# Context values of four heads in one run of products, tokens on partitions

## The chip, the cores and the metric

The kernel runs on one core of one Trainium2 chip. The metric is the device time of one execution in microseconds (us). The kernel before took 2483.2 us, the median of 3 runs (2482.09 to 2486.21).

## What is computed

One post-norm decoder layer in float32 over x of 8 batches x 100 tokens x 1024 features: a retention block, a cross attention over the layer's own tokens and a context of 722 tokens a batch, and a gated feed-forward block, each followed by a residual sum and a layer norm. The change lies in the cross attention, of which this is the core:

```python
q = (x @ wq).reshape(B, L, 16, 128)
k = (x @ wk).reshape(B, L, 4, 128)
v = (x @ wv).reshape(B, L, 4, 128)
k_ctx = (h_ctx_kv @ wk_ctx).reshape(B, 722, 4, 128)
v_ctx = (h_ctx_kv @ wv_ctx).reshape(B, 722, 4, 128)
...
k_full = jnp.concatenate([k_ctx, k], axis=1)
v_full = jnp.concatenate([v_ctx, v], axis=1)
scores = jnp.einsum('blhd,bmhd->bhlm', q, k_full) * scale + mask
probs = jax.nn.softmax(scores, axis=-1)
out = jnp.einsum('bhlm,bmhd->blhd', probs, v_full)
```

Four query heads share one of the four key/value heads, so keys and values are repeated four times ahead of the scores. Keys and queries are also RMS-normalised, and own queries and keys rotated.

## The kernel before

Activations lie with features on the 128 partitions and tokens along the row. Every float32 operand of a product is kept as a high part and a low part in the type fp32r, and `mm3` (L89) makes a product of three matmuls: high x high (L90), high x low (L93) and low x high (L94). `split2` (L67) makes the two parts: ScalarE (ACT) copies into fp32r and VectorE (DVE) subtracts, both on L68. `proj` (L113) multiplies a 128-column block of weights by all 8 blocks of features: 24 matmuls into one bank of PSUM. Banks come by tag: three of `a`, four of `s`, one of `v` (L51).

The program is written as a sequence; a scheduler then sets the order of instructions on each engine, from a timeline of its own, with the buffers of the pools as limits. A tile with `bufs=1` can be written again only when all its readers are done. On each engine the order is then fixed.

Stage one is the retention block. At its side `core` (L538) prepares the weights of the context for all later batches: `wc` holds, by turns, the key and value weights of the four heads; each is split into high and low part and kept in DRAM as `wcd` (1 MB each, L565 by SP's queue; L566 adds on POOL's queue, to complete the low part).

A stage of queries, own keys and own values follows, and at its side the context of batch 0 is loaded and the context keys of heads 0 and 1 of batch 0 are made (`early`, L723 to L759). The queries are kept in `qd`, the own keys in `kd`, the own values in `vd`.

Then comes the loop that the change is in, over 8 batches `b` and 4 key/value heads `kv` (L773 to L870). For one batch:

- `load_context` (L689) loads the context in 8 pieces (`cs`, 3 buffers) and splits them into four tiles `cz`, in two halves of 362 and 360 tokens (`SH`, L21). The four tiles hold the context of one batch; the next batch's come in when the last product has read them.
- `context_keys` (L693): one head's weights by `load_ws` (L82, tag `w`, four buffers of 1 MB), a product for each half, ACT's square (L705), POOL's sum over partitions (L706, 2.4 us), and the split into `kall`, which has two buffers. The sums go to DRAM as a row (L710) and come back as a column (L800); L802 to L809 make from it a scale `rk` for each context token.
- `context_values` (L713): one head's weights, a product for each half with features on partitions, copied out of PSUM (L719, once by ACT and once by DVE), turned by TensorE in six transposes (L794), and split into `vall` (L796), two tiles that heads use by turns. Own values come in behind the context's (L785, L786).
- The scores (L821) for 822 keys in seven chunks c of 128 keys with 4 x 100 queries along the row, in the order 6, 5, 0, 1, 2, 3, 4; chunk 5 is the context's last 82 keys and the first own ones, chunk 6 the own rest. ACT (L828) or DVE (L824) scale them into `s`; DVE takes the maximum over chunks (L829, L832) and POOL over partitions (`all_red`, L833).
- The softmax: DVE subtracts the maximum (L839, L843), ACT takes the exponential (L845), `split2` makes `ph` and `pl`, DVE sums over chunks (L848, L851), and POOL over partitions (L852). `s`, `ph` and `pl` have one buffer each.
- The context product (L858): 21 matmuls into bank `v` with `vall` as weights; then the division by the sum (L862 to L867), a split and a store to `o2d` (L870).

After the loop `out_proj` (L238) multiplies by the output weights, in two halves of the batches, adds the residual and normalises. Its first half (batches 0 to 3) can begin before the loop's end. Its tile `y` and its residual tiles `rs` are in pool `y2`, which opens before the loop (L764).

Of the kernel before, what the change touches and what calls it, by code (L numbers as in the profile page):

```python
# [8 lines left out]
F32 = mybir.dt.float32  # L9
FR = mybir.dt.float32r  # L10
AF = mybir.ActivationFunctionType
ALU = mybir.AluOpType
# [4 lines left out]
P = 128  # L17
B, T, D = 8, 100, 1024
NB = 4
N = NB * T  # L20
KT = D // P  # L21
QT = KT // 2
SC, SH = 722, 362
SN = [SH, SC - SH]
NC = 7
ORDER = (6, 5, 0, 1, 2, 3, 4)
C5 = SC - 5 * P
R6 = SC + T - 6 * P
# [3 lines left out]
NKV = 4  # L32
# [8 lines left out]
def decoder_layer(ctx, tc, xT, cT, w1, wo1, w2, wo2, wc, w3, wd, gw, qw, kw, trig, dec, mask, out):  # L41
    nc = tc.nc

    def sbuf(name, bufs, side=None):
        return tc.tile_pool(name=name, bufs=bufs, side=side, reuse_waits="tile")
# [8 lines left out]
    def bank(tag):  # L54
        return ps.tile([P, 512], F32, tag=tag, name=tag, bufs=banks[tag])

    def f32(ap):
        return ap.bitcast(F32)

    def bt(ap):  # L60
        return ap.rearrange("p (b t) -> p b t", b=NB)
# [5 lines left out]
    def split2(hi, lo, src):  # L67
        return nc.scalar.copy(hi, src), nc.vector.tensor_tensor(lo, src, f32(hi), ALU.subtract)  # L68
# [10 lines left out]
            split(w, st)  # L79
        return w  # L80

    def load_ws(i):  # L82
        w = wp.tile([P, 2, KT * P], FR, tag="w", name="w", bufs=4)
        nc.sync.dma_start(out=f32(w), in_=f32(wcd[i]))
        return w

    pin = tc.keep_in_program_order
# [1 line left out]
    def mm3(acc, lh, ll, rh, rl, start, stop, chain=False, pinned=False):  # L89
        i = nc.tensor.matmul(acc, lh, rh, start=start, stop=False, skip_group_check=chain)  # L90
        if pinned:
            pin(i)
        nc.tensor.matmul(acc, lh, rl, start=False, stop=False, skip_group_check=chain)  # L93
        nc.tensor.matmul(acc, ll, rh, start=False, stop=stop, skip_group_check=chain)  # L94
# [18 lines left out]
    def proj(w, z, n=N, tag="a", todo=None, pinned=False):  # L113
        acc = bank(tag)[:, :n]
        first = pinned
        for k in range(KT):
            pinned = between(todo, k) or first and k == 0
            t = z[k // QT]
            mmw(acc, w, k, t[:, 0, k % QT, :n], t[:, 1, k % QT, :n], k == 0, k == KT - 1, pinned)
        return acc  # L120
# [53 lines left out]
    o2d = dr.tile([B, P, NKV, 4, 2, T], FR, name="o2d")  # L174
    zd = dr.tile([2, P, KT, N], F32, name="zd")
    zd2 = dr.tile([2, P, KT, N], F32, name="zd2")
    wcd = dr.tile([2 * NKV, P, 2, KT * P], FR, name="wcd")
    hd = dr.tile([QT - 1, 7, P, 2, QT, N], FR, name="hd")
    h3d = dr.tile([4, P, 2, QT, N], FR, name="h3d")

# [296 lines left out]
    with sbuf("l1", 2) as p:  # L477
# [60 lines left out]
        def core(h):  # L538

            for half in range(2):  # L540
                q, k = qk[half, 0], qk[half, 1]
                pf = p.tile([T, NB, T], F32, tag="pf", name="pf")
                s = bt(bank("v")[0:T, :N])
                for b in range(NB):
                    e = slice(b * T, (b + 1) * T)
                    nc.tensor.matmul(s[:, b], k[:, e], q[:, e], start=True, stop=True)
                nc.vector.tensor_tensor(pf, s, dcy[:, h, None, :].to_broadcast([T, NB, T]), ALU.mult)
                ot = p.tile([P, 2, N], F32, tag="ot", name="ot")
                sq = p.tile([P, 2, N], F32, tag="sq", name="sq", bufs=1)
                for blk in range(2):  # L550
                    vv = v[half, blk]
                    o = bank("s")[:, :N]
                    for b in range(NB):
                        nc.tensor.matmul(bt(o)[:, b], vv[:, b * P:(b + 1) * P], pf[:, b], start=True, stop=True)  # L554
                    nc.scalar.activation(ot[:, blk], o, AF.Copy, scale=gws[:, blk:blk + 1])
                    nc.scalar.activation(sq[:, blk], o, AF.Square)
                nc.vector.tensor_tensor(sq[:, 0], sq[:, 0], sq[:, 1], ALU.add)
                oo[half], ss[half] = ot, all_red(p, sq[:, 0], "ss")


            w = wp.tile([P, 2, KT * P], FR, tag="w", name="w", bufs=4)
            st = load_raw(wc[h])
            nc.scalar.copy(w[:, 0], st)
            nc.scalar.activation(w[:, 1], f32(w[:, 0]), AF.Copy, scale=-1.0)
            nc.sync.dma_start(out=f32(wcd[h]), in_=f32(w))  # L565
            nc.gpsimd.dma_start(out=f32(wcd[h])[:, 1], in_=st, accum_op=ALU.add)  # L566

        def gated(h, g):

# [97 lines left out]
    cz = []  # L667
# [21 lines left out]
    def load_context(b):  # L689
        for _ in context_steps(b, wp, 3):  # L690
            pass

    def context_keys(kv):  # L693

        kall = ka.tile([P, 2, SC + T], FR, tag="kall", name="kall")
        wk = load_ws(2 * kv)
        sq = ka.tile([P, SC], F32, tag="ksq", name="ksq", bufs=1)
        ss = ka.tile([P, 6 * P], F32, tag="kss", name="kss", bufs=1)
        row = dr.tile([6, P], F32, tag="row", name="row", bufs=2)
        nc.gpsimd.memset(ss[:, SC:], 1.0)  # L700

        def step(hf):
            n, at = SN[hf], slice(hf * SH, hf * SH + SN[hf])
            acc = proj(wk, cz[hf], n)
            nc.scalar.activation(sq[:, at], acc, AF.Square)  # L705
            nc.gpsimd.partition_all_reduce(ss[:, at], sq[:, at], P, RED.add)  # L706
            nc.scalar.activation(kall[:, 0, at], acc, AF.Copy, scale=kws)
            nc.vector.scalar_tensor_tensor(kall[:, 1, at], acc, kws, f32(kall[:, 0, at]), ALU.mult, ALU.subtract)
            if hf:
                nc.sync.dma_start(out=row.rearrange("c p -> (c p)")[None, :], in_=ss[0:1])  # L710
        return step, (kall, row)

    def context_values(kv):  # L713

        wv = load_ws(2 * kv + 1)
        vt = ka.tile([P, SC], F32, bufs=1, tag="cvt", name="cvt")
        for hf in range(2):
            copy = nc.scalar.copy if hf == 0 else nc.vector.tensor_copy
            copy(vt[:, hf * SH:hf * SH + SN[hf]], proj(wv, cz[hf], SN[hf]))  # L719
        return vt  # L720


    early = []  # L723
    behind = list(behind)
    groups = [[(kv, 5) for kv in range(NKV)]]
    for kv in range(NKV):
        groups += [[(kv, i) for i in range(2)], [(kv, i) for i in range(2, 5)]]
    unit = NKV
    with sbuf("l2", 2) as p:
        ctx0 = context_steps(0, p, 2, behind)  # L730
# [30 lines left out]
    z1pool.__exit__(None, None, None)  # L761


    y2pool = sbuf("y2", 1)  # L764
    y2p = y2pool.__enter__()
    with sbuf("cx", 2) as p, sbuf("c1", 1) as p1:

        ph = p1.tile([P, NC, N], FR, name="ph")
        pl = p1.tile([P, NC, N], FR, name="pl")
        valls = [p1.tile([P, NC, 2, P], FR, name=f"vall{i}") for i in range(2)]  # L770
        for t in [ph[:, 0], pl[:, 0]] + [v[:, 6] for v in valls]:
            nc.gpsimd.memset(f32(t), 0.0)
        for b in range(B):  # L773
            if b > 0:
                load_context(b)
            for kv in range(NKV):
                if early:
                    kall, row = early.pop(0)
                else:
                    step, (kall, row) = context_keys(kv)  # L780
                    step(0)
                    step(1)
                nc.sync.dma_start(out=f32(kall[:, :, SC:]), in_=f32(kd[kv, :, b]))
                vall = valls[kv % 2]
                nc.sync.dma_start(out=f32(vall[C5:P, 5]), in_=f32(vd[kv, 0:P - C5, b]))  # L785
                nc.sync.dma_start(out=f32(vall[0:R6, 6]), in_=f32(vd[kv, P - C5:T, b]))  # L786
                q = p.tile([P, 4, 2, T], FR, tag="q", name="q")
                nc.sync.dma_start(out=f32(q).rearrange("p h l t -> p h (l t)"),
                                  in_=f32(qd[kv, :, :, b]).rearrange("h p l t -> p h (l t)"))
                vt = context_values(kv)  # L790
                for c0, c1, rows in ((0, 3, P), (3, 5, P), (5, 6, C5)):
                    tr = bank("s")
                    for c in range(c0, c1):
                        nc.tensor.transpose(tr[0:rows, (c - c0) * P:(c - c0 + 1) * P], vt[:, c * P:c * P + rows], ident)  # L794
                    src = tr[0:rows, 0:(c1 - c0) * P].rearrange("p (c d) -> p c d", d=P)
                    split2(vall[0:rows, c0:c1, 0], vall[0:rows, c0:c1, 1], src)  # L796

                rr = p.tile([P, 6], F32, tag="rr", name="rr")
                with nc.allow_non_contiguous_dma("a row turned into a column"):
# [8 lines left out]
                nc.vector.scalar_tensor_tensor(rk[:, 0:5], r1[:, 0:5], 3.0, r0[:, 0:5], ALU.subtract, ALU.mult)  # L808
                nc.vector.scalar_tensor_tensor(rk[0:C5, 5:6], r1[0:C5, 5:6], 3.0, r0[0:C5, 5:6], ALU.subtract, ALU.mult)  # L809

                s = p1.tile([P, NC, N], F32, tag="s", name="s")
                mx = p.tile([P, N], F32, tag="mx", name="mx")
                def part(ap, c):
                    ap = bt(ap)
# [39 lines left out]
                for j in (1, 0, 2, 3, 4, 5, 6):  # L854
                    c = ORDER[j]
                    n = N6 if c == 6 else N
                    o = bt(ov)[:, :, T6:] if c == 6 else bt(ov)
                    mm3(o, vall[:, c, 0], vall[:, c, 1], bt(ph[:, j, :n]), bt(pl[:, j, :n]),  # L858
                        j == 1, j == NC - 1)

                r = p.tile([P, N], F32, bufs=1, tag="r0", name="r0")
# [10 lines left out]
    def load_o2(half):  # L872
# [4 lines left out]
                in_=f32(o2d[half * NB:(half + 1) * NB, :, g]).rearrange("b p h l t -> p b (h l t)"))  # L877
        return lambda k: (t[k // 4][:, :, k % 4, 0], t[k // 4][:, :, k % 4, 1])

    kapool.__exit__(None, None, None)  # L880


# [384 lines left out]
```

## Time and profile before

| | before |
|---|---|
| median of 3 runs | 2483.2 us |
| profiled execution | 2485.66 us |
| its span | 2483.9 us |
| TensorE clock granted | 0.997 of full |
| loop over batches and heads, first to last softmax | some 832 to 1604 us of the span |
| VectorE busy over the span | 79% |
| ScalarE busy over the span | 54% |
| GpSimd busy over the span | 19% |

The span is from the first to the last instruction; the rest of the execution's time lies around it. In lines of instructions the name left of the arrow is written and those right of it are read; a number in square brackets is the time that the engine stood idle before the instruction, with what ended it. Matmuls are pipelined: one is shown with 0.33 us though the next starts after half of that, so a price is read from one start to the next. PE is TensorE, SP the queue that issues most DMAs. In a table by windows the columns are the stretch, its length, then busy time and instructions of PE, PE's weight loads, DVE, ACT and POOL, the granted clock, the share of the DMA engines and GB/s.

### The profile page before, as it was taken

What the parts mean: (1) busy time and instruction counts of PE and PEld (TensorE: products, weight loads), DVE (VectorE), ACT (ScalarE), POOL (GpSimd) and SP (SyncE); (2) the same over time, 40 slices, a digit from 0 to 9 for tenths busy, and PEclk for the clock granted to TensorE, in tenths of its full rate; (3) what the DMA queues carried; (4) which work ended last, traced back from release to release, by engine and by line L of the source; (5) the groups of instructions that cost most, each with busy time, mean ns of one, the idle gap of its engine ahead of it and who ended that gap; (6) DMA issues with size and microseconds to landing.
All of it is one profiled execution on the core that took longest, in us unless ns stands there. A gap on an engine that the chain in (4) does not pass through costs nothing.

```text
span 2483.9 us, 37221 instructions
## 1 busy us (share of the span) xinstructions
PE 2459.2 (99%) x14068; PEld 2440.1 (98%) x14068; DVE 1953.3 (79%) x3101; ACT 1340.1 (54%) x2258; POOL 460.2 (19%) x234
## 2 busy tenths in 40 slices
PE   9999999999999999999999999999999999999997
PEld 9999999999999999999999999999999999999997
DVE  7777877566898698998998999748978777666756
ACT  6667676334888465666566656534545445432221
POOL 0111111000565333443443433100000000000000
PEclk9999999999999999999999999999999999999999
DMA  7333445775544555455555454565445444389731
GB/s 244 112 111 129 134 141 185 247 261 181 164 161 157 182 175 168 144 181 159 160 174 159 152 181 168 165 241 178 154 174 194 163 161 161 121 301 324 267 103 54
DMA packets 224451, 433.98 MB, mean 175 GB/s; under 512 B 47338, under 2 KB 168042, under 8 KB 211854
## 3 DMA queue, kind: packets, MB, share of 16 engines
q1 hardware_dynamic: 222542, 426.87, 51.2%
q0 software_dynamic: 1152, 4.19, 1.1%
q8 instruction: 111, 1.82, 0.3%
q14 instruction: 70, 0.57, 0.1%
q10 hardware_dynamic: 576, 0.52, 0.1%
HBM read 322.18 MB, written 109.35 MB: 174 GB/s over the span
## 4 chain that ended last, share of the span: by engine, by line
PE 93%; DVE 3%; DMA 2%; ACT 1%; issue 1%; SPq 0%; DVEq 0%; ACTq 0%
PE a L94 20%; PE a L93 20%; PE a L90 20%; PE s L94 9%; PE s L93 9%; PE s L90 9%; PE v L94 2%; PE v L90 2%; PE v L93 1%; PE s L554 1%; PE s L794 1%; PE s L166 1%; DVE y L331 0%; DMA cs<-in_cT 0%; DMA rs<-zd 0%
## 5 line engine op out<-in xcount | busy, mean ns | idle before, releaser
L90 PE MATMUL a<-big,w 128*128 128x400 f32 (+2 forms) x1808 | 609.8, 338 | 0.9 <-DVE y L424 0.7
L93 PE MATMUL a<-big,w 128*128 128x400 f32 (+2 forms) x1808 | 609.2, 337 | 0.2 <-DVE big L68 0.2
L94 PE MATMUL a<-big,w 128*128 128x400 f32 (+2 forms) x1808 | 608.0, 337 | 0.6 <-DVE w L68 0.6
L68 ACT CAST w<-wst 128x1024 fp32r<-128x1024 f32 (+1 forms) x231 | 239.6, 1039 | 386.2 <-PE s L94 146.0
L68 DVE TENSOR_TENSOR w<-wst,w 128x1024 fp32r<-128x1024 f32 (+1 forms) x231 | 280.6, 1215 | 135.0 <-ACT w L68 133.0
L90 PEld LDWEIGHTS a<-big,w 128*128 128x128 f32 x1808 | 340.0, 188 | 2.4 <-DVE y L424 1.0
L93 PEld LDWEIGHTS a<-big,w 128*128 128x128 f32 x1808 | 340.5, 188 | 1.6 <-DVE big L68 0.4
L94 PEld LDWEIGHTS a<-big,w 128*128 128x128 f32 x1808 | 340.7, 189 | 1.5 <-DVE w L68 0.9
L90 PE MATMUL a<-z,w 128*128 128x400 f32 x680 | 234.7, 345 | 0.4 <-ACT w L68 0.4
L93 PE MATMUL a<-z,w 128*128 128x400 f32 x680 | 234.7, 345 | 0.0
L94 PE MATMUL a<-z,w 128*128 128x400 f32 x680 | 234.5, 345 | 0.0
L90 PE MATMUL s<-big,w 128*128 128x400 f32 x664 | 230.0, 347 | 0.1
L94 PE MATMUL s<-big,w 128*128 128x400 f32 x664 | 228.9, 346 | 0.4 <-DVE w L68 0.4
L93 PE MATMUL s<-big,w 128*128 128x400 f32 x664 | 229.2, 345 | 0.0
L141 POOL PARTITION_ALL_REDUCE ss<-sq x56 | 148.4, 2651 | 325.8 <-DMA vd<-vs 185.6
L706 POOL PARTITION_ALL_REDUCE kss<-ksq x64 | 166.1, 2596 | 125.3 <-ACT ksq L705 124.6
L828 ACT ACTIVATE s<-s,rk 128x400 f32<-128x400 f32 x160 | 88.1, 591 | 101.1 <-DVE sm L848 66.7
L90 PEld LDWEIGHTS a<-z,w 128*128 128x128 f32 x680 | 127.6, 188 | 1.2 <-ACT w L68 0.8
L94 PEld LDWEIGHTS a<-z,w 128*128 128x128 f32 x680 | 128.4, 189 | 0.0
L93 PEld LDWEIGHTS a<-z,w 128*128 128x128 f32 x680 | 127.6, 188 | 0.4
L90 PEld LDWEIGHTS s<-big,w 128*128 128x128 f32 x664 | 124.6, 188 | 1.7 <-ACT w L68 0.4
L94 PEld LDWEIGHTS s<-big,w 128*128 128x128 f32 x664 | 125.1, 188 | 0.7 <-DVE w L68 0.7
(355 smaller groups left out, 5444.4 us busy)
## 6 DMA issues: line engine op xcount, KB each, us to landing
wst<-in_w SPq DMA_DIRECT2D x135, 512.0 KB
w<-wcd SPq DMA_DIRECT2D x64, 1024.0 KB
wst<-in_wo SPq DMA_DIRECT2D x64, 512.0 KB
hd<-h SPq DMA_DIRECT2D x12, 1400.0 KB
wst<-in_wd SPq DMA_DIRECT2D x64, 256.0 KB
big<-o1d SPq DMA_DIRECT2D x16, 800.0 KB
qd<-d SPq DMA_DIRECT2D x32, 400.0 KB
q<-qd SPq DMA_DIRECT2D x32, 400.0 KB
```

The source lines that it names most:

```text
L68: return nc.scalar.copy(hi, src), nc.vector.tensor_tensor(lo, src, f32(hi), ALU.subtract)
L90: i = nc.tensor.matmul(acc, lh, rh, start=start, stop=False, skip_group_check=chain)
L93: nc.tensor.matmul(acc, lh, rl, start=False, stop=False, skip_group_check=chain)
L94: nc.tensor.matmul(acc, ll, rh, start=False, stop=stop, skip_group_check=chain)
L141: nc.gpsimd.partition_all_reduce(y, x, P, op)
L166: nc.tensor.transpose(tr[0:T, b * P:(b + 1) * P], vt[:, b * T:(b + 1) * T], ident)
L554: nc.tensor.matmul(bt(o)[:, b], vv[:, b * P:(b + 1) * P], pf[:, b], start=True, stop=True)
L706: nc.gpsimd.partition_all_reduce(ss[:, at], sq[:, at], P, RED.add)
L794: nc.tensor.transpose(tr[0:rows, (c - c0) * P:(c - c0 + 1) * P], vt[:, c * P:c * P + rows], ident)
L828: nc.scalar.activation(sc, sp, AF.Copy, scale=rk[:, c:c + 1])
```

## The change

The values of the context are made for all four heads of a batch at once, before the first head. For each chunk of 128 context tokens the context is the stationary operand and the value weights of the four heads, side by side, are the moving one: 8 blocks of features x 3 matmuls with 512 columns fill one bank with tokens on partitions and four heads x 128 features along the row. The split goes from there into `vall`; there is no copy and no transpose. For this

- the two halves of the context become 384 and 338 tokens, so that a half holds three whole chunks;
- stage one writes the value weights of a head into `wvd`, with the four heads of a feature block next to each other, in runs of 128 values; the key weights stay in `wcd`, four of them;
- a batch loads its value weights as four tiles, each with two feature blocks of all four heads, in the four buffers of tag `w`; the key weights of head 0 come into a buffer of their own, `wk`;
- `vall` is one tile for the four heads of a batch, 28672 bytes a partition, where there were two with 7168 each;
- pool `y2` opens after the loop, not before it;
- the last pair of groups of the stage before runs in the opposite order, and `s` is taken once before the loop.

```diff
-SC, SH = 722, 362
+SC, SH = 722, 384
...
-    def load_ws(i):
-        w = wp.tile([P, 2, KT * P], FR, tag="w", name="w", bufs=4)
-        nc.sync.dma_start(out=f32(w), in_=f32(wcd[i]))
+    def load_ws(src, w=None):
+        if w is None:
+            w = wp.tile([P, 2, KT * P], FR, tag="w", name="w", bufs=4)
+        nc.sync.dma_start(out=f32(w), in_=f32(src))
         return w
...
-    wcd = dr.tile([2 * NKV, P, 2, KT * P], FR, name="wcd")
+    wcd = dr.tile([NKV, P, 2, KT * P], FR, name="wcd")
+    wvd = dr.tile([P, 2, KT, NKV, P], FR, name="wvd")
...
-            nc.sync.dma_start(out=f32(wcd[h]), in_=f32(w))
-            nc.gpsimd.dma_start(out=f32(wcd[h])[:, 1], in_=st, accum_op=ALU.add)
+            if h % 2 == 0:
+                to, wf, low = f32(wcd[h // 2]), f32(w), st
+            else:
+
+                to, wf = f32(wvd)[:, :, :, h // 2], f32(w).rearrange("p l (k n) -> p l k n", n=P)
+                low = st.rearrange("p (k n) -> p k n", n=P)
+            nc.sync.dma_start(out=to, in_=wf)
+            nc.gpsimd.dma_start(out=to[:, 1], in_=low, accum_op=ALU.add)
...
-    def context_values(kv):
-
-        wv = load_ws(2 * kv + 1)
-        vt = ka.tile([P, SC], F32, bufs=1, tag="cvt", name="cvt")
-        for hf in range(2):
-            copy = nc.scalar.copy if hf == 0 else nc.vector.tensor_copy
-            copy(vt[:, hf * SH:hf * SH + SN[hf]], proj(wv, cz[hf], SN[hf]))
-        return vt
+    def context_values(vall):
+
+        wv = [load_ws(wvd[:, :, 2 * j:2 * j + 2].rearrange("p l k v n -> p l (k v n)")) for j in range(QT)]
+        for c in range(NC - 1):
+            rows, hf, at = C5 if c == 5 else P, c // 3, c % 3 * P
+            acc = bank("a")[0:rows, :NKV * P]
+            for k in range(KT):
+                zh, zl = (cz[hf][k // QT][:, l, k % QT, at:at + rows] for l in range(2))
+                wh, wl = (wv[k // 2][:, l, k % 2 * NKV * P:(k % 2 + 1) * NKV * P] for l in range(2))
+                mm3(acc, zh, zl, wh, wl, k == 0, k == KT - 1)
+            split2(vall[0:rows, c, :, 0], vall[0:rows, c, :, 1], acc.rearrange("p (v d) -> p v d", d=P))
...
-        groups += [[(kv, i) for i in range(2)], [(kv, i) for i in range(2, 5)]]
+        pair = [[(kv, i) for i in range(2)], [(kv, i) for i in range(2, 5)]]
+        groups += pair[::-1] if kv == NKV - 1 else pair
...
-        valls = [p1.tile([P, NC, 2, P], FR, name=f"vall{i}") for i in range(2)]
+        vall = p1.tile([P, NC, NKV, 2, P], FR, name="vall")
...
             if b > 0:
                 load_context(b)
+            context_values(vall)
             for kv in range(NKV):
                 if early:
                     kall, row = early.pop(0)
                 else:
-                    step, (kall, row) = context_keys(kv)
+                    w = p1.tile([P, 2, KT * P], FR, tag="wk", name="wk") if kv == 0 else None
+                    step, (kall, row) = context_keys(kv, w)
...
-                vall = valls[kv % 2]
-                nc.sync.dma_start(out=f32(vall[C5:P, 5]), in_=f32(vd[kv, 0:P - C5, b]))
-                nc.sync.dma_start(out=f32(vall[0:R6, 6]), in_=f32(vd[kv, P - C5:T, b]))
+                nc.sync.dma_start(out=f32(vall[C5:P, 5, kv]), in_=f32(vd[kv, 0:P - C5, b]))
+                nc.sync.dma_start(out=f32(vall[0:R6, 6, kv]), in_=f32(vd[kv, P - C5:T, b]))
...
-                vt = context_values(kv)
-                for c0, c1, rows in ((0, 3, P), (3, 5, P), (5, 6, C5)):
-                    tr = bank("s")
-                    for c in range(c0, c1):
-                        nc.tensor.transpose(tr[0:rows, (c - c0) * P:(c - c0 + 1) * P], vt[:, c * P:c * P + rows], ident)
-                    src = tr[0:rows, 0:(c1 - c0) * P].rearrange("p (c d) -> p c d", d=P)
-                    split2(vall[0:rows, c0:c1, 0], vall[0:rows, c0:c1, 1], src)
...
-                    mm3(o, vall[:, c, 0], vall[:, c, 1], bt(ph[:, j, :n]), bt(pl[:, j, :n]),
+                    mm3(o, vall[:, c, kv, 0], vall[:, c, kv, 1], bt(ph[:, j, :n]), bt(pl[:, j, :n]),
```

More of the change, by code (lines that the diff above doesn't have):

```diff
@@ L691, in load_context, with context_keys @@
             pass
-    def context_keys(kv):
+    def context_keys(kv, w=None):
         kall = ka.tile([P, 2, SC + T], FR, tag="kall", name="kall")
-        wk = load_ws(2 * kv)
+        wk = load_ws(wcd[kv], w)
         sq = ka.tile([P, SC], F32, tag="ksq", name="ksq", bufs=1)
@@ L761, in decoder_layer @@
     z1pool.__exit__(None, None, None)
-    y2pool = sbuf("y2", 1)
-    y2p = y2pool.__enter__()
     with sbuf("cx", 2) as p, sbuf("c1", 1) as p1:
+        s = p1.tile([P, NC, N], F32, tag="s", name="s")
         ph = p1.tile([P, NC, N], FR, name="ph")
         pl = p1.tile([P, NC, N], FR, name="pl")
-        valls = [p1.tile([P, NC, 2, P], FR, name=f"vall{i}") for i in range(2)]
-        for t in [ph[:, 0], pl[:, 0]] + [v[:, 6] for v in valls]:
+        vall = p1.tile([P, NC, NKV, 2, P], FR, name="vall")
+        for t in [ph[:, 0], pl[:, 0], vall[:, 6]]:
             nc.gpsimd.memset(f32(t), 0.0)
@@ L809, in decoder_layer @@
                 nc.vector.scalar_tensor_tensor(rk[0:C5, 5:6], r1[0:C5, 5:6], 3.0, r0[0:C5, 5:6], ALU.subtract, ALU.mult)
-                s = p1.tile([P, NC, N], F32, tag="s", name="s")
+                if b + kv > 0:
+                    s = p1.tile([P, NC, N], F32, tag="s", name="s")
                 mx = p.tile([P, N], F32, tag="mx", name="mx")
@@ L878, in load_o2 @@
         return lambda k: (t[k // 4][:, :, k % 4, 0], t[k // 4][:, :, k % 4, 1])
+    y2pool = sbuf("y2", 1)
+    y2p = y2pool.__enter__()
     kapool.__exit__(None, None, None)
```

## The prediction

> **What bounds the kernel now.** First the busy shares and the chain that ended last: TensorE (PE) carries both. Then one batch of cross attention, from the timeline of VectorE (DVE), and the busy time in it by engine.
>
> ```profile
> PE 2459.2 (99%) x14068; PEld 2440.1 (98%) x14068; DVE 1953.3 (79%) x3101; ACT 1340.1 (54%) x2258; POOL 460.2 (19%) x234
> PE 93%; DVE 3%; DMA 2%; ACT 1%; issue 1%; SPq 0%; DVEq 0%; ACTq 0%
> ```
> ```profile
> 1028.50:1123.10 94.60, 94.60 (x575) 93.99 (x574) 88.20 (x154) 58.60 (x112) 37.46 (x20) 1.00 0.51 164
> ```
> ```profile
> 1009.13 0.37 DVE L824 SCALAR_TENSOR_TENSOR s<-s,msk 54x216 f32<-54x216 f32 x1
> ...
> 1018.80 0.37 DVE L839 TENSOR_TENSOR s<-s,mb 54x216 f32<-54x216 f32 x1
> ...
> 1028.52 0.36 DVE L824 SCALAR_TENSOR_TENSOR s<-s,msk 54x216 f32<-54x216 f32 x1
> ...
> 1049.31 0.37 DVE L824 SCALAR_TENSOR_TENSOR s<-s,msk 54x216 f32<-54x216 f32 x1
> ...
> 1103.76 0.37 DVE L824 SCALAR_TENSOR_TENSOR s<-s,msk 54x216 f32<-54x216 f32 x1
> ```
>
> Over 94.6 us PE (first column) has no gap, and DVE (third) is busy 88.2. Each L824 on 54x216 opens a head's softmax, so two quiet heads took 19.4 and 20.8 us and four heads 94.6 (1009.13 to 1103.76). A head cannot overlap the next: `s`, `ph` and `pl` have one buffer. PE stays full because values and keys of the next head stand in those 20 us.
>
> **PE's prices** are start-to-start distances, since durations overlap:
>
> ```profile
> 1010.75 0.35 PE L93 MATMUL s<-q,kall 128*128 128x400 f32 x1
> 1010.94 0.35 PE L94 MATMUL s<-q,kall 128*128 128x400 f32 x1
> ...
> 1011.49 0.35 PE L94 MATMUL s<-q,kall 128*128 128x400 f32 x1
> 1011.67 0.49 PE L794 MATMUL s<-ident,cvt 128*128 128x128 f32 x3
> 1011.92 0.41 PE L93 MATMUL a<-big,w 128*128 128x360 f32 x1
> 1012.17 0.32 PE L94 MATMUL a<-big,w 128*128 128x360 f32 x1
> 1012.33 0.33 PE L90 MATMUL a<-big,w 128*128 128x360 f32 x1
> ```
>
> 400 columns cost 0.183 us (mean of such runs), 360 or 362 cost 0.1655, 216 cost 0.10. Three transposes and a 360 fill 1011.67 to 1012.17, so a transpose costs (0.50-0.165)/3 = 0.112.
>
> **The change, part by part.** *Products.* Per batch 4x2x24 = 192 matmuls of 361 become 6x24 = 144 of 512. No row has 512: by proportion 512x0.183/400 = 0.2346, by the slope between 361 and 400, 0.00045 a column, 0.2333; I take 0.2346, as 216 lies near the proportion too. So 33.8 for 31.8 us; 24 transposes go, -2.7. Keys (384+338 columns for 362+360) stay at 31.8, scores and context products at 4x(36x0.183+6x0.10) = 28.8. PE's work per batch falls from 95.1, which is the trace's 94.6 to 95.3 with no gap, to 94.4: -0.7, or -6 us over eight.
>
> The Trainium skill, "TensorE: Matmul & The Clock Gate", section "Back-to-back issue gap", puts a warm gap at N/2.4+2.5 ns: 169 at 400, where this trace has 183. By it 512 would cost 216, an estimate, and PE's work would fall by 27 us instead of 6.
>
> *DVE and ScalarE.* Per batch 12 L68 subtractions into `vall` (0.46+0.27+0.26 a head) and four L719 copies (0.45) go, six 128x512 subtractions come (128x384 is 0.46 start to start, so 0.62): 5.8 becomes 3.7. DVE keeps 86 of 94 us.
>
> *Stage one.* Four value weights are written in 512-byte runs and added by POOL's queue, 1024 pieces where there were 128. The issue L566 took 0.88 us and landed in 6.2; eight times each is 7 and 50. Rows there show POOL waiting 261 us on these transfers and PE 99.8% busy, so I price it 0; uncovered it would delay a head's all-reduce by some 10 us.
>
> *Order.* This decides. The built order of the changed kernel has per batch, on PE: values of chunks 3-5; keys of head 0; keys 1 with scores 0; keys 2 and 3; context product (AV) of head 0; values 0-2 of the next batch with scores 1; AV1; scores 2, 3; AV2; rest of scores 3; AV3; and only then values 3-5. `vall` now has one buffer, read by all four AVs, so the split of a value bank waits for AV3; three value chunks hold the three `a` banks until then, and keys need those too. From AV1 to AV3 PE has 2x7.2+3.7 = 18 us of work while DVE does two softmaxes, 35 us. After AV3, PE does values 3-5 and keys 0 alone, while DVE waits. Behind the waiting splits on DVE stand the last L848 and the all-reduce of its sum; behind value chunk 3 on PE stand keys 0 and scores 0, for which DVE waits. On SP the `vall<-vd` loads wait for AV, with context loads behind; and the fourth value weight waits for keys 3.
>
> **The sum, one batch,** from the last L848 of head 3 (0) to that of the next batch. Rows for the keys' scale:
>
> ```profile
> 1062.26 0.47 ACT L705 ACTIVATE ksq<-a 128x360 f32<-128x360 f32 x1 [2.43 <-PE a L94]
> ...
> 1062.82 2.38 POOL L706 PARTITION_ALL_REDUCE kss<-ksq  x1 [1.24 <-ACT ksq L705]
> ...
> 1065.23 0.24 SPq L710 DMA_DIRECT2D row<-kss  x1
> 1066.92 0.37 SPq L800 DMA_DIRECT2D rr<-row  x1
> ...
> 854.58 0.30 ACT L802 ACTIVATE rr<-rr,eps_k 128x6 f32<-128x6 f32 x1 [1.45 <-DMA rr<-row]
> ```
>
> Tail of AV3 1.5 (six matmuls, PE at half pace, below); values 3-5 72x0.2346 = 16.9; keys 0 48x0.1655 = 7.9: at 26.3. Scale: square and reduce 2.9 (1062.26 to 1065.20), with 0.3 before; write to read 1.7; read 2.3 (issued 852.28, used 854.58); then 2.0 of small operations (L802 to L809 took 817.46 to 819.84 once, with other work between): 35.5. Maximum and its all-reduce: 9.7 (1009.13 to 1018.80) less 2.0 for two L708 and three `vall` subtractions: 43.2. Exponentials of head 0: 9.7 (to 1028.52) less 0.9 (L719, scale) = 8.8, plus four context subtractions at 0.9, a key subtraction 0.5, 0.4 scale, 0.7 waiting for keys 3: 57.2. Head 1: a bare head is 19.4-2.95 = 16.5 or 20.8-2.95 = 17.8, say 17, plus four context subtractions 3.4, keys 1.0, scale 0.4: 79.0. Heads 2 and 3: 17 and 18, one for half pace: 114. PE's 94.4 lie inside, 20 idle.
>
> Half pace has a row: after 3.4 us without a matmul the scores start 0.333 apart until 839.
>
> ```profile
> 829.78 0.33 PE L93 MATMUL a<-big,w 128*128 128x362 f32 x1
> 833.22 0.70 PE L90 MATMUL s<-q,kall 128*128 128x400 f32 x1 [3.11 <-DVE s L824]
> ...
> 836.99 0.54 PE L90 MATMUL s<-q,kall 128*128 128x400 f32 x1
> 837.32 0.54 PE L93 MATMUL s<-q,kall 128*128 128x400 f32 x1
> ```
>
> The skill's same page ("Why this matters for your kernels") forbids idle gaps over some 3 us for this; the row agrees. It speaks against this change, whose gaps before AV2 and AV3 are longer.
>
> Seven such cycles: batch 0's last sum ended at 930.7, batch 7's at 1604.2, 673.5 in all; now 7x114 = 798: +124.5. Batch 0: 0 (its keys 0 and 1 are ready; -5 to +10 for four 1 MB value weights at once). At the end 234 products of the output projection were done before the last AV, 192 now: 42x0.183 = +7.7. Its `y` comes into the softmax pools' room, so PE waits with full banks for the last head's division and a 200 KB load: +5 (0 to 9). Total +137: on the profiled 2485.7 (span 2483.9) 2623; the runs' median is 2.5 lower, so 2620.
>
> Bounds of a cycle: 107 (heads at 16.5, -2.5; no AV tail, -1.5; quick scale reads, -1.7; no waits for context or at half pace, -1.3) and 121 (heads at 17.8, +3; scale transfers up to the 3.4 and 4.5 us seen elsewhere, +4). So 76-5 to 174+10, plus 7.7 and 0 to 9: 2560 to 2685.
>
> **Rivals.** *Covered* (4%), the other side: its place is PE's 25 us behind AV3 (values 3-5, keys 0). If a chunk's split into `vall` may run once AV3 has read that chunk, and PE gets ahead of DVE, they fall into heads 2 and 3, a cycle is PE's 94.4, and the gain is 0.7 a batch: -6 us (-7 by the slope), 2476 to 2478. It decides once a cycle's 20 idle us are below 0.7. For: PE is 93% of the chain. Against: AV3 stands before values 3-5 in a fixed order and needs the last `pl`. *Level* (2%): a cycle of 95 to 96, 2479 to 2488; it would need bare heads at 12 us, and the two rows give 16.5 and 17.8. *Late weights* (7%): the fourth value weight and the last context pieces, queued behind waits on SP, arrive late; AV1 then waits too. Each us per cycle is 7; from 8 late (cycle 122) it decides: 2685 to 2740. Against: 5 MB move in about 20 us, 250 GB/s, and slices with 301 to 324 GB/s exist. *The change not doing what it says*, values spread among heads as before, is excluded by the built order.
>
> My forecast has 87%. Faster by over 0.2% (what a measurement here can tell from no change) 0.04, within 0.02, slower 0.94. The range leaves out late weights and covered.
>
> **What would show it.** PE idle of some 20 us a batch, mostly ended by DVE `pl` (L68), and clock below 1.00 there; L830 to L830 (old L824) about 17 to 18 in heads 2 and 3; 40 us or more from a batch's last sum to the next L845 (old L839); 512-column matmuls 0.23 apart. Wrong if PE stays full across a batch boundary or cycles are under 105.

## The result, and the profile after

The changed kernel took 2672.3 us (median of 4 runs, 2669.2 to 2672.9) against 2484.7 us for the kernel before on the same chip: a ratio of 1.0755, 95% interval 1.0741 to 1.0769. The profiled execution took 2672.0 us, its span 2670.2 us.

The busy shares and the chain that ended last, of the changed kernel:

```profile
PE 2496.0 (93%) x13492; PEld 2404.4 (90%) x13492; DVE 1934.7 (72%) x3021; ACT 1329.0 (50%) x2178; POOL 484.9 (18%) x233
PE 76%; DVE 13%; DMA 5%; issue 3%; ACT 2%; POOL 0%; SPq 0%; POOLq 0%; DVEq 0%; ACTq 0%
```

PE had 99% of the span and 93% of the chain; it now has 93% and 76%, and the difference went to DVE (13%) and to DMAs (5%). No engine took PE's place: DVE fell from 79% to 72%.

One batch, from its predecessor's last sum to its own, and the longest waits of PE (us in total, times, longest):

```profile
1053.30:1172.00 118.70, 99.99 (x509) 90.68 (x509) 84.58 (x144) 57.45 (x103) 40.73 (x20) 0.92 0.40 131
```
```profile
PE v L91 <- DVE sm L854: 116.5, 14, 10.3
PE a L91 <- DVE kall L716: 10.9, 8, 2.5
```

118.7 us where there were 94.6, with PE idle in 18.7 of them and the clock at 0.92. Fourteen times, twice in each of the first seven batches, a context product (bank `v`) waited for a softmax: these are the gaps ahead of the products of heads 2 and 3. The same batch on DVE (L830 was L824, L845 was L839, L854 was L848):

```profile
1052.74 0.56 DVE L854 TENSOR_TENSOR sm<-sm,s 128x400 f32<-128x400 f32 x1
...
1053.82 0.36 DVE L830 SCALAR_TENSOR_TENSOR s<-s,msk 54x216 f32<-54x216 f32 x1
...
1087.62 0.64 DVE L830 SCALAR_TENSOR_TENSOR s<-s,rk,msk 128x400 f32<-128x400 f32 x1
...
1096.48 0.62 DVE L716 SCALAR_TENSOR_TENSOR kall<-a,kws,kall 128x384 fp32r<-128x384 f32 x1 [2.68 <-ACT kall L715]
1097.79 0.17 DVE L810 TENSOR_TENSOR rr<-rr 128x6 f32<-128x6 f32 x1 [0.69 <-ACT rr L808]
1097.88 0.37 DVE L845 TENSOR_TENSOR s<-s,mb 54x216 f32<-54x216 f32 x1
...
1135.68 0.38 DVE L830 SCALAR_TENSOR_TENSOR s<-s,msk 54x216 f32<-54x216 f32 x1
...
1153.70 0.38 DVE L830 SCALAR_TENSOR_TENSOR s<-s,msk 54x216 f32<-54x216 f32 x1
...
1171.42 0.56 DVE L854 TENSOR_TENSOR sm<-sm,s 128x400 f32<-128x400 f32 x1
```

After the last sum (1053.3) DVE scales chunk 6 of head 0's scores at once, for it holds own keys alone and needs no `rk`. Then DVE has no scores for 33 us: those of chunk 5, the first to need `rk`, come at 1087.62, and the maximum is subtracted at 1097.88. What PE did meanwhile:

```profile
1047.58 0.70 PE L91 MATMUL v<-ph,vall 128*128 128x400 f32 x1 [9.80 <-DVE sm L854]
...
1053.41 0.54 PE L94 MATMUL v<-pl,vall 128*128 128x400 f32 x1
1053.74 0.54 PE L95 MATMUL v<-ph,vall 128*128 128x400 f32 x1
...
1054.57 0.34 PE L95 MATMUL v<-ph,vall 128*128 128x400 f32 x1
1054.75 0.40 PE L91 MATMUL a<-w,big 128*128 128x512 f32 x1
...
1070.89 0.39 PE L95 MATMUL a<-w,big 128*82 128x512 f32 x1
1071.12 0.33 PE L91 MATMUL a<-big,wk 128*128 128x384 f32 x1
```

A gap of 10 us, then the last context product, at half pace (0.33 us apart at 1053.41) until 1054; then values 3-5, 16.1 us, and only then the keys of head 0. PE and DVE, which were busy side by side for 94.6 and 88.2 us of a batch's 94.6, now take turns at the batch boundary.

`vall` is freed chunk by chunk, not as a whole: ACT wrote the next batch's chunk 0 as soon as the last context product had read the old one, 3.6 us before that product's last matmul (1054.57). What holds values 3-5 back is thus that this product, the last of the batch, begins to read only in head 3's softmax (1047.58).

```profile
1050.98 0.59 ACT L68 CAST vall<-a 128x512 fp32r<-128x512 f32 x1 [1.17 <-PE v L94]
```

The whole difference in span, 2670.2 - 2483.9 = 186.3 us, lies in three places. Seven cycles (batches 1 to 7, each from last sum to last sum): 833.3 for 673.4, +159.9. Batch 0's last sum: 934.6 for 930.8, +3.8. From the last sum to the end: 902.4 for 879.7, +22.7.

### The profile page after: what moved, and what is told of

It reads as the page before. It is cut to its first block, busy times and chain, and to the rows that moved or that the text cites. A ratio compares the mean times of both kernels' runs of the same rounds, so it can differ in the third digit from the quotient of the medians.

```text
span 2670.2 us, 35938 instructions
## 1 busy us (share of the span) xinstructions
PE 2496.0 (93%) x13492; PEld 2404.4 (90%) x13492; DVE 1934.7 (72%) x3021; ACT 1329.0 (50%) x2178; POOL 484.9 (18%) x233
## 3 DMA queue, kind: packets, MB, share of 16 engines
q1 hardware_dynamic: 234318, 426.87, 47.6%
## 4 chain that ended last, share of the span: by engine, by line
PE 76%; DVE 13%; DMA 5%; issue 3%; ACT 2%; POOL 0%; SPq 0%; POOLq 0%; DVEq 0%; ACTq 0%
PE a L95 17%; PE a L91 17%; PE a L94 16%; PE s L95 7%; PE s L94 7%; PE s L91 7%; DVE sm L854 2%; DVE pl L68 2%; DVE s L849 2%; DVE mx L835 1%; PE v L94 1%; PE v L95 1%; PE s L556 1%; PE v L91 1%; DMA rr<-row 1%
## 5 line engine op out<-in xcount | busy, mean ns | idle before, releaser
L91 PE MATMUL a<-big,w 128*128 128x400 f32 (+2 forms) x1184 | 404.3, 342 | 12.4 <-DVE y L272 9.7
L95 PE MATMUL a<-big,w 128*128 128x400 f32 (+2 forms) x1184 | 402.7, 340 | 0.5 <-DVE w L68 0.4
L94 PE MATMUL a<-big,w 128*128 128x400 f32 (+2 forms) x1184 | 402.4, 340 | 0.2 <-DVE big L68 0.2
L91 PEld LDWEIGHTS a<-big,w 128*128 128x128 f32 x1184 | 223.3, 189 | 15.4 <-DVE y L272 10.0
L95 PEld LDWEIGHTS a<-big,w 128*128 128x128 f32 x1184 | 223.6, 189 | 1.1 <-DVE w L68 1.1
L94 PEld LDWEIGHTS a<-big,w 128*128 128x128 f32 x1184 | 223.2, 189 | 0.9 <-DVE big L68 0.4
L714 POOL PARTITION_ALL_REDUCE kss<-ksq x64 | 175.0, 2734 | 212.1 <-ACT ksq L713 212.0
L91 PE MATMUL v<-ph,vall 128*128 128x400 f32 (+1 forms) x224 | 91.5, 408 | 119.3 <-DVE sm L854 116.5
L91 PEld LDWEIGHTS v<-ph,vall 128*128 128x128 f32 x224 | 52.7, 235 | 124.7 <-ACT ph L68 124.3
L91 PE MATMUL a<-w,big 128*128 128x512 f32 (+1 forms) x384 | 151.8, 395 | 12.1 <-DVE kall L716 10.2
L95 PE MATMUL a<-w,big 128*128 128x512 f32 (+1 forms) x384 | 150.4, 392 | 0.0
L94 PE MATMUL a<-w,big 128*128 128x512 f32 (+1 forms) x384 | 150.3, 391 | 0.0
L142 POOL PARTITION_ALL_REDUCE mb<-sm x32 | 87.6, 2739 | 272.4 <-DVE sm L854 260.8
```

The costliest lines, as they stand in the source:

```text
L142: nc.gpsimd.partition_all_reduce(y, x, P, op)
```

## The experiments

"Cycle" is the mean of batches 2 to 6, "boundary" the time from a batch's last sum to the first subtraction of the next maximum (into batches 2 and 3), "tail" the time from the last sum to the end of the span. values_once leaves out the context's values of batches 1 to 7; all others do the whole computation.

| kernel | us | ratio to the kernel before (95%) | boundary | cycle | tail |
|---|---|---|---|---|---|
| before | 2483 to 2485 | | 10.6 to 11.1 | 95.0 | 879.7 |
| the change | 2672.3 | 1.0755 (1.0741 to 1.0769) | 43.4 to 44.6 | 118.5 | 902.4 |
| values_once | 2512.1 | one run | 8.5 | 95.7 | 900.3 |
| keys_first | 2599.3 | 1.0466 (1.0448 to 1.0483) | 21.8 to 22.6 | 107.0 | 900.4 |
| scores_first | 2584.1 | 1.0401 (1.0386 to 1.0417) | 9.7 to 10.6 | 107.4 | 900.2 |
| warm | 2696.6 | 1.0852 (1.0836 to 1.0868) | 47.1 to 47.6 | 122.1 | 902.7 |
| spare0 | 2702.2 | 1.0879 (1.0860 to 1.0899) | 42.4 to 44.1 | 124.3 | 898.8 |
| spare3 | 2593.9 | 1.0442 (1.0425 to 1.0458) | 24.7 to 29.3 | 109.3 | 900.0 |
| spare3_keys | 2534.2 | 1.0202 (1.0187 to 1.0217) | 13.8 to 14.3 | 98.8 | 900.7 |
| no_wk | 2683.9 | 1.0810 (1.0792 to 1.0828) | 43.5 to 43.7 | 120.3 | 901.1 |
| pairs | 2492.7 | 1.0040 (1.0024 to 1.0056) | 10.3 to 11.9 | 94.5 | 899.7 |
| before_y2 | 2495.9 | 1.0053 (1.0037 to 1.0069) | 11.2 to 13.5 | 95.6 | 899.2 |
| pairs_y2 | 2507.7 | 1.0096 (1.0081 to 1.0111) | 10.7 to 11.3 | 94.6 | 905.1 |
| pairs_best | 2969.9 | 1.1953 (1.1937 to 1.1969) | 25.5 to 25.7 | 158.4 | 890.7 |

### Without the work: values once

```diff
-            context_values(vall)
+            if b == 0:
+                context_values(vall)
```

> Leaves out the values of the context of batches 1 to 7: batch 0's values serve all of them. Measured with the change: 118.7 us a batch, 44.5 of it from a batch's last sum to the first subtraction of the maximum (L845). Theory (a serial chain sets the cycle; at the boundary PE makes values 3-5 and keys 0 while VectorE waits): the 17 us of values 3-5 leave the boundary, so about 27 us there and a cycle of 99 to 103; 7 cycles give 110 to 138 us, the whole about 2535 to 2560. Rival (the 144 wide products themselves are the load, PE's work sets the cycle): a cycle loses all 144x0.227 = 33 us and comes to 86, the whole about 2440. Second rival (the clock or late loads set it): a cycle stays above 110.

The window 1080 to 1300 of this kernel and of the change:

```profile
1080.00:1300.00 220.00, 172.55 (x851) 157.28 (x850) 199.94 (x316) 123.03 (x224) 112.23 (x48) 0.87 0.40 119
```
```profile
1080.00:1300.00 220.00, 183.33 (x925) 166.79 (x924) 167.72 (x281) 111.33 (x199) 78.52 (x39) 0.91 0.39 123
```

The cycle fell to 95.7, between what the theory (99 to 103) and the rival (86) expected; neither had its number. Taking out 144 x 0.227 = 33 us of PE's work gave 23. PE now stands idle for a fifth of the time, and DVE is busy for 200 of 220 us: the softmax chain by itself takes about 95 us a batch, by this one run. The boundary fell to 8.5, not to 27, since the keys of head 0 went into the softmax too (products with `wk` from 1052 to 1082, where batches end at 1042 and 1141). So the kernel before had two chains of about 95 us each, PE's and the softmax's, side by side, with little slack in either: where one waits for the other, not much of the wait is made up.

### Moving the block: keys first, scores first

```diff
             if b > 0:
                 load_context(b)
-            context_values(vall)
...
                     step(1)
+                if kv == 0:
+                    context_values(vall)
```

> Same computation; in the order of the program the values of a batch stand behind the keys of head 0 and not ahead of them. Theory (values 3-5 wait for the last context product, and keys 0 stand behind them without a reason of their own): keys 0 fall into the softmax of heads 1 to 3, their sums and scale are done by the end of the last product, and values 3-5 still stand ahead of most of scores 0. The boundary falls from 44.5 to 21 to 32 us, the cycle to 95 to 106, the whole to 2510 to 2590. Rival (wide products set the time by themselves): same cycle of 118 and 2672, since PE's work is unchanged.

In the second one the same line stands behind the loop over scores, ahead of `all_red(p, mx, "mb", RED.max)`.

> Same computation; the values of a batch stand behind head 0's scores in the order of the program. Theory: what values 3-5 wait for then holds up nothing that VectorE needs, the 17 us are done during head 0's softmax, the boundary falls to 20 us or less and the cycle to PE's 94 to 98; the loss that is left is the end (+22.7) and the first batch (+3.9): 2495 to 2540. Rival (one buffer of vall holds the cycle wherever the values stand): context product 0 has to wait for values 3-5, the cycle stays above 106 and the whole above 2590. Rival (wide products cost more than narrow ones): a cycle above 100 with PE full.

Both boundaries came out as expected (22 and 10 us), and in neither did the cycle: 107.0, and 107.4 where 95 to 106 and 94 to 98 were expected. With the keys first the boundary that is left, 11 us longer than in the kernel before, is about the whole of the loss in a cycle. With the scores first the wait moved; on DVE (L829 was L824 of the kernel before):

```profile
1160.49 1.17 DVE L855 TENSOR_TENSOR sm<-sm,s 128x400 f32<-128x400 f32 x2
1161.77 0.38 DVE L829 SCALAR_TENSOR_TENSOR s<-s,msk 54x216 f32<-54x216 f32 x1
...
1179.83 0.17 DVE L809 TENSOR_TENSOR rr<-rr 128x6 f32<-128x6 f32 x1 [2.11 <-ACT rr L807]
...
1180.63 0.63 DVE L829 SCALAR_TENSOR_TENSOR s<-s,rk,msk 128x400 f32<-128x400 f32 x1
```

Head 0 is through at 1161.7, and head 1 finds no scale `rk` until 1180.4: values 3-5 now stand ahead of head 1's keys and of context product 0. Head 1 takes 46 to 48 us where it took 28 in the kernel before. The rival that set the cycle above 106 had this one right, though the whole stayed below its 2590. In all three places of the block, 16 us of products fall between the last context product of one batch and the first of the next, where DVE has one head to work on; and PE still waits 7.2 us ahead of the product of head 3. Even so the two moves took 73 and 88 us of the change's 188 away.

### The half clock: warm

Products of constants fill the gaps ahead of the context products of heads 2 and 3.

```diff
                 ov = bank("v")[:, :N]
+                for _ in range((0, 0, 28, 38)[kv]):
+                    nc.tensor.matmul(ov[:, 0:P], onem, onem, start=True, stop=True)
```

> Same computation, with added products of 128x128 constants into the bank of the context product, 28 ahead of head 2's and 38 ahead of head 3's, to fill the gaps of 7.4 and 9.7 us after which the granted clock falls to half for 6.8 to 13.7 us. Theory (half clock costs only where PE is on the chain: end of the last context product and part of values 3-5): 1.5 to 4 us a cycle, the whole 10 to 30 us less than the changed kernel, 2640 to 2662. Rival (the half clock is the main loss of the boundary): 8 to 10 us a cycle, 2600 to 2615. If the added products stand in the way of work instead: above 2672.

It became 24 us slower: the added products had to wait for bank `v` (5.0 us in the first row below, which holds the 38 of head 3, two rows each) and ran past the time at which the softmax was ready. The context product of head 3 began 9.5 us after the first subtraction of the maximum (L845, 1046.14), in the change 3.9 (1162.38 to 1166.26). The total says nothing of the clock, but values 3-5 do, which ran at full clock here:

```profile
1045.12 10.77 PE L861 MATMUL v<-onem 128*128 128x128 f32 x76 [5.00 <-DVE ofs L875]
1055.64 0.43 PE L91 MATMUL v<-ph,vall 128*128 128x400 f32 x1
...
1059.33 0.40 PE L91 MATMUL a<-w,big 128*128 128x512 f32 x1
...
1075.47 0.39 PE L95 MATMUL a<-w,big 128*82 128x512 f32 x1
```

16.14 us, as in the change (1054.75 to 1070.89). The half clock had passed there when values 3-5 began; what it slows is the last context product. In the change the last `pl` was ready at 1051.7, and six matmuls of 0.183 us behind it would end at 1052.8, where values 3-5 began at 1054.75. So a full clock could give at most some 2 us a cycle at the boundary. This is an estimate from these rows, not shown by a gain.

### Room for the values: spare chunks

`vall` is cut into a tile for each chunk, in turn among six or nine buffers; the own values of chunk 6 have their own. To make room the key weights of head 0 use tag `w`, the square of the keys has half the columns and the division is done in place.

```diff
-        vall = p1.tile([P, NC, NKV, 2, P], FR, name="vall")
+        vall = {6: p1.tile([P, NKV, 2, P], FR, name="vown")}
+        def chunk(c):
+            vall[c] = p1.tile([P, NKV, 2, P], FR, tag="vall", name="vall", bufs=SPARE + NC - 1)
+            return vall[c]
```

> Same computation as the change; vall is cut into chunk tiles (six used in turn, a seventh for the own values), the key weights of head 0 use tag w, and two scratch tiles are smaller. It is the partner of the kernel with three spare chunks. Theory and rival alike: cutting the tile changes nothing, since all chunks are read by the last context product within 4 us; cycle 116 to 121, the whole 2655 to 2690.

> As the partner, with nine chunk tiles in turn, not six: three spare ones. Theory (values 3-5 stand behind the last context product for want of room alone): values 0-2 of the next batch leave the three banks early, values 3-5 follow in the softmax of heads 2 and 3, where PE is idle. The boundary falls from 44.5 by values 3-5's 16 us to 27 to 30, the cycle from 118.7 to 101 to 106, the whole by 90 to 125 to 2550 to 2585. Rival (the wide products or the chain on VectorE set the cycle wherever the values stand): less than 30 us from its partner.

Three buffers of 4096 bytes a partition took 108 us off (2702.2 to 2593.9), within the 90 to 125 expected: values 3-5 now run between the context products of heads 1 and 2, and the boundary fell by 15 to 18. The cycle (109.3) and the whole lay above what was expected, since spare0 was itself 30 us slower than the change. Of these 30, the missing buffer `wk` explains 12:

```diff
-                    w = p1.tile([P, 2, KT * P], FR, tag="wk", name="wk") if kv == 0 else None
+                    w = None
```

> The change without the buffer wk: the key weights of head 0 use the four buffers of tag w, behind the four value tiles. It tells whether the 30 us between the change (2672) and the kernel cut into six chunk tiles (2702) are this buffer, and what late weights cost. Theory (they are): cycle 122 to 126, the whole 2695 to 2710. Rival (the cut into chunk tiles cost it): within 8 us of 2672.

2683.9 stands between theory and rival, with a cycle of 120.3. The other 18 us (the cut, or the smaller scratch tiles) weren't told apart. Spare chunks and the keys of head 0 ahead of the values, together:

> As the kernel with three spare chunks, with the values behind the keys of head 0 in the order of the program. Theory (with room for the chunks and head 0's keys done early, nothing on PE's side is left in the boundary but scores 0): boundary 10 to 18, cycle from 108.1 to 95 to 102, the whole 2500 to 2555. Rival (values 0-2 still wait for room, and context product 0 for values 3-5): cycle 104 or more, the whole above 2565.

2534.2, cycle 98.8, as the theory had it. The same window of spare0, spare3 and spare3_keys, with PE busy for 178, 198 and 212 of 220 us at a clock of 0.90, 0.94 and 0.98:

```profile
1080.00:1300.00 220.00, 177.88 (x895) 161.67 (x893) 159.65 (x262) 105.10 (x190) 80.69 (x39) 0.90 0.39 126
```
```profile
1080.00:1300.00 220.00, 197.80 (x1017) 181.18 (x1016) 166.70 (x285) 114.71 (x206) 80.64 (x41) 0.94 0.45 142
```
```profile
1080.00:1300.00 220.00, 212.35 (x1115) 193.62 (x1114) 198.47 (x321) 126.51 (x232) 101.84 (x45) 0.98 0.50 163
```

### The form without the lump: pairs

Values with tokens on partitions and no transposes, for two heads at a time, in two tiles used by turns (together as large as `vall`). The second pair's values stand behind the keys of head 2, and the key weights of head 0 use tag `w`.

```diff
-            acc = bank("a")[0:rows, :NKV * P]
+            acc = bank("a")[0:rows, :2 * P]
...
-        vall = p1.tile([P, NC, NKV, 2, P], FR, name="vall")
+        valls = [p1.tile([P, NC, 2, 2, P], FR, name=f"vall{i}") for i in range(2)]
...
+                if kv == 0:
+                    context_values(vall, 0)
...
+                if kv == 2:
+                    context_values(vall, 1)
```

> Same computation: values with tokens on partitions and no transposes, as in the change, but for two heads at a time (256 columns), with two half-size tiles used in turn by pairs; together they take the same 28672 bytes a partition. Theory (the form is innocent; one tile for four heads is what costs): half of the values can be made while the other pair's softmax runs, PE stays full or nearly, cycle 95 to 100; with the end's +22.7 and the first batch's +3.9 the whole 2505 to 2550. Rival (the form costs by itself, by its moving operand or its splits): cycle above 106, the whole above 2590.

```profile
1080.00:1300.00 220.00, 220.00 (x1510) 219.61 (x1509) 202.72 (x346) 129.62 (x253) 96.73 (x45) 1.00 0.53 169
```

In the same window PE has no gap and the clock is full: a cycle of 94.5, the loop 671.4 us for 673.4 before, the whole 2492.7, below the range expected. The form is innocent. So are stage one's writes of value weights in 512-byte runs: this kernel makes them too, and its batch 0 ends at 921.9. What cost 160 us is one buffer for four heads, with the order that it forces. This kernel by itself doesn't show it, for the width of the products and the place of half of them differ too; but spare3_keys keeps the 512 columns, and its cycle of 98.8 leaves them some 4 us a cycle at most.

### The end: the pool of y

The kernel before, with this alone of the change:

```diff
-    y2pool = sbuf("y2", 1)
-    y2p = y2pool.__enter__()
     with sbuf("cx", 2) as p, sbuf("c1", 1) as p1:
...
+    y2pool = sbuf("y2", 1)
+    y2p = y2pool.__enter__()
     kapool.__exit__(None, None, None)
```

> The kernel before with one part of the change alone: the pool with y and the residual tiles opens after the loop. 192 products of the output projection then stand before the last context product, as in the change, where there were 234. Theory (the end's +22.7 of the change is all from this pool: 42 products x 0.183 = 7.7, a stall of 10, and half clock behind it): 15 to 23 us more than before, 2499 to 2508, and the loop as before (673.5). Rival (the end of the change is longer because of its values and weights): within 8 us of before.

The products behind the last context product, first in this kernel, then in the change:

```profile
1605.74 0.70 PE L90 MATMUL a<-big,w 128*128 128x400 f32 x1 [10.80 <-DVE y L270]
```
```profile
1778.82 0.70 PE L91 MATMUL a<-big,w 128*128 128x400 f32 x1 [9.66 <-DVE y L272]
1779.32 0.54 PE L94 MATMUL a<-big,w 128*128 128x400 f32 x1
1779.66 0.54 PE L95 MATMUL a<-big,w 128*128 128x400 f32 x1
```

PE stands 10 to 11 us with full banks, for `y` has no room until the softmax pools close, and begins again at half pace (0.34 us from 1779.32 to the next). The tail grew by 19.5 (899.2 for 879.7), so nearly all of the change's +22.7 is this pool. The whole grew by only 12.9, less than expected: batch 0's last sum came 7.5 us earlier (923.3 for 930.8) with the pool out of the way. The other way round, the kernel with pairs and the pool early again:

> As the kernel with values by pairs of heads, with the pool of y opened before the loop again; room for it comes from smaller scratch tiles, one residual tile where there were two, and the last mixing tiles in another pool. 212 products of the output projection stand before the last context product (192 there, 234 in the kernel before). Theory (the form costs nothing, the end is the pool's): the gap of 11.3 us after the last context product goes and 20 x 0.183 = 3.7 move ahead of it, 2492.7 - 10 to 15 + 0 to 7 for the first batch, which was 8 earlier with the pool late: 2478 to 2490, the kernel before at best beaten by a few us. Rival (one residual tile, or the tiles moved, bring a stall of their own): above 2495.

The gap behind the last context product was gone, but with one residual tile the last six sums of the projection each waited 0.7 to 3.1 us for their load, and the kernel was 15 us slower than pairs. One such sum on DVE, and the two longest waits of PE:

```profile
1703.27 0.57 DVE L272 TENSOR_TENSOR y<-a,rs 128x400 f32<-128x400 f32 x1 [2.35 <-DMA rs<-zd]
```
```profile
PE s L360 <- DVE s L316: 11.6, 1, 11.6
PE s L91 <- ACT s L958: 10.6, 1, 10.6
```

The first of them, 2.8 us in pairs, follows from these sums. The second stands behind the mixing that comes next, with DVE busy and waiting for no load; its cause isn't shown. With two residual tiles, and for that one scratch tile shared by the keys' square and the division:

```diff
-                r = p.tile([P, N], F32, bufs=1, tag="r0", name="r0")
+                r = ka.tile([P, N], F32, bufs=1, tag="ksq", name="r0")
```

> As the kernel with values by pairs and y's pool opened before the loop, with both residual tiles again (the division of the context product and the keys' square share one scratch tile instead). The earlier one had no gap after the last context product, but a residual load behind every sum (gap of 12.0 us ahead of the mean, and 10.9 once more behind it). 334 products of the output projection stand before the last context product, 234 in the kernel before. Theory (pool order and residual tiles set the end, not the values): tail after the last sum 875 to 885 us, where pairs with the pool late had 899.7; loop 671 to 676; the whole 2473 to 2484, at or a little below the kernel before. Rival (the mixing tiles in the other pool, or the shared scratch tile, bring the stall back): 2490 or more.

2969.9, a cycle of 158. ACT in this kernel, the square of a head's keys behind the division of the head before:

```profile
1117.19 0.52 ACT L68 CAST oh<-r 128x400 fp32r<-128x400 f32 x1 [2.00 <-DVE r L879]
1118.36 0.49 ACT L713 ACTIVATE ksq<-a 128x384 f32<-128x384 f32 x1 [0.64 <-DVE oh L68]
...
1127.68 0.30 ACT L813 ACTIVATE rr<-rr,eps_k 128x6 f32<-128x6 f32 x1 [5.31 <-DMA rr<-row]
```

One shared tile of 1600 bytes puts keys, sums, row and scale of each head behind the previous head's division: the change's own mechanism, once a head where the change has it once a batch. No version beat the kernel before. Pairs came nearest, 0.4% slower, its tail still 20 us longer; whether it would win with `y` early, two residual tiles and no shared scratch stays open.

## Why the prediction was right, point by point

Slower, by 188 us where 137 was forecast: inside the range, 13 us from its upper end. The misses all point one way: the seven cycles +35, the end +10, batch 0 +4.

- *The order decides; `vall` has one buffer.* Right, and shown from both sides: spare chunks took the boundary down, and two half tiles brought it back to that of the kernel before.
- *The cycle, 114.* The mechanism was right, the size small: 118.7 in the cycle shown, piece by piece:

| piece | forecast | measured (1053.3 to 1172.0) |
|---|---|---|
| AV tail, values 3-5, keys 0, scale, to chunk 5's scores | 35.5 | 34.3 |
| maximum and all-reduce | 7.7 | 10.3 |
| head 0's exponentials | 14.0 | 14.4 |
| head 1 | 21.8 | 23.3 |
| head 2 | 17 | 18.1 |
| head 3 | 18 | 18.4 |

 The largest miss is the maximum. The working took out 2.0 for operations that fall away; but on DVE the subtraction now stands behind a key split of head 2 and the scale of head 1, with 2.7 and 0.7 us of idle time ahead of them (1096.48 and 1097.79), and that scale waited for its sums to come back from DRAM. It is a term mis-sized by 2.6; the heads add 3.4 and the scale gives back 1.2. The sum over the loop was short besides: seven equal cycles of 114 were set against 673.5 us before, which hold a longer last cycle (100.7, with output weights to prepare). The last cycle was the longest after the change too, 122.2. So 833 us, not 798.
- *512 columns, 0.2346.* Measured 16.14/71 = 0.2273. The rule of the Trainium skill ("TensorE: Matmul & The Clock Gate", "Back-to-back issue gap"), 216 ns at 512 columns, is nearer to it than it was at 400 columns (169 against 183), but no run here reached it. PE's work is then 144 x 0.0073 = 1.1 us a batch below the forecast, 1.8 below the kernel before; a cycle in which PE waits for 18.7 us can't show it.
- *Half pace.* It was there, 0.333 us apart, and by the estimate above it cost at most some 2 us a cycle. (The 3.4 us that the prediction read ahead of its row are from start to start; the row has 3.11 of idle time.) The skill's same page ("Why this matters for your kernels") forbids gaps over some 3 us for it; here the gap itself, 10 us, was the loss, and filling it to keep the clock made things slower.
- *The end, 7.7 + 5.* 42 products did move; the stall was 10 us, not 5 nor at most 9, and half pace behind it (18 products, 0.15 more each) and a second gap of 1.5 us took most of the rest of 22.7. This is the term furthest off in proportion.
- *Batch 0, 0.* +3.8, in two parts that were not seen: 7.5 earlier for the pool (before_y2), and so some 11 later for the rest, which is put down to six chunks of values ahead of head 0. With the values behind head 0's scores its last sum came at 924.4, 10.2 earlier.
- *Late weights*, a rival, fell for the change: PE waited for value weights three times in the whole execution, 1.7 us in all. Without `wk` a weaker form of it appears, 12 us in all. *Covered* and *level* fell by the boundary of 44 us.
- *The signs.* PE's idle time (18.7 us a batch), the clock (0.92), heads 2 and 3 (18.0 and 18.8 from L830 to L830), the boundary (44 us) and 0.227 us a matmul came as announced, or nearly. One did not: the profile names the sum `sm` (L854, 116.5 us) as what ended PE's waits for context products, and `pl` for 7.4 us.

## What to carry to other kernels

When two engines' chains are equally long, a buffer that all users of a round share turns overlap into taking turns; ask of each enlarged tile who must be done before its first piece can be written again, and what other work there is for PE and for DVE in that time. Here moving the block in the program took less than half of the loss away and left the wait in another place; room for half the tile took about half, and half-size tiles by turns at the same bytes took all of it out of the loop. Where a tile is given up to make room for another (`y`'s pool, `wk`, one residual tile, a shared scratch tile), price that too: here each cost from 12 to over 450 us.

## What the runs showed that was not expected

Products of 256 (pairs), 400 (before) and 512 columns (the change) stood 0.120, 0.183 and 0.227 us apart, so the cost per column falls slightly with width (0.47, 0.46 and 0.44 ns), and wide products save about 3% against proportion from 400 columns. After a gap of 10 us the half pace lasted over 6 us (from 1047.58 to after 1053.74), longer than the product it fell on needs at full pace.
